# A perceiver layer on Trainium2: later tails' values half a section on, last output product half a step on, seven products of ones, root first

## The chip, the cores and the metric

The kernel runs on one core of a Trainium2 chip (trn2). All arithmetic is fp32. The metric is the device time in microseconds (us), median of three runs. Beside it there is one profiled execution, in which the hardware profiler records the instructions of each engine. The engines are TensorE (PE: matmuls, and PEld: its weight loads), VectorE (DVE), ScalarE (ACT), GpSimd (POOL) and SyncE (SP), which only issues DMAs here. ACT and POOL issue DMAs too, besides their own work.

## The reference

One layer in three stages, each on a layer norm of the running rows x (8 batches x 64 queries, 512 wide) and added to them:

```python
def stablemax(s):
    s = where(s >= 0, s + 1, 1 / (1 - s))
    return s / s.sum(-1)

# 1: cross attention, 16 heads of 32, context of 8 x 1601 rows of 512
n = layernorm(x)
q, k, v = n @ Wq.T + bq, ctx @ Wk.T + bk, ctx @ Wv.T + bv
x = x + (stablemax(q @ k.T / sqrt(32)) @ v) @ Wo.T + bo
# 2: causal self attention over 64 rows, 8 query heads of 64, one shared key and value
n = layernorm(x)
x = x + softmax(causal(n @ aWq @ (n @ aWk).T * 512**-0.5)) @ (n @ aWv) @ Wp + bp
# 3: experts, 512 -> 2048 -> 512
n = layernorm(x)
shared = mean over 2 of gelu(n @ sW1 + sb1) @ sW2 + sb2
gates = n @ rW + rb        # top 2 of 8, softmax over the two
x = x + shared + sum over the top 2 of w_e * (gelu(n @ W1[e] + b1[e]) @ W2[e] + b2[e])
```

## The kernel before

**Context.** The keys and values of the 8 x 1601 context rows are the larger part of the work. Each batch has three *sections* of 512 rows (24 in all, numbered 0 to 23), 64 further rows (its *tail*) and one last, *odd* row. A product of two 2x2 block matrices is made with seven block products instead of eight: `weight_parts` (L353, on DVE) makes the sums of weight blocks, `context_part` and `tail_parts` those of the context blocks (POOL), `multiply` (L370, its matmul is L376) issues one of the seven, and `products` (L382) returns the seven as *units*. A unit ends with a copy from PSUM on ACT (through a helper that keeps ACT's order, so the profile gives L87), a join on DVE (L405) or, for the fifth, an add on POOL (L448). The first section's keys are plain products (`first_keys`, L465).

**Tails.** They are taken for four batches at a time, because four tails of 64 rows fill a tile of 256. Half 0 (batches 0 to 3) is made at the start; half 1 after section 14, the last of batch 4. `load_tails` (L183) loads the context, `tail_parts` makes the block differences, `tail_products` (L536) returns the units: key units `ku`, value units `vu`, and the last value unit `last`, which also writes the values to a scratch in DRAM (`vt_d`, L559, on SP). `load_vt` (L568) reads a batch's values back when its scores begin. `odd_rows` (L501) and `odd_turn` (L522) make key and value of the odd rows; `odd_k` is filled by four ACT activations that add the key bias.

**The order of work.** `Plan` (L52) holds units, each with a planned length, and other steps, each with a planned time. The units run through: sections (loop at L1124), first expert, further expert blocks. Steps such as loading a section, scores and weighing of a tile of context are put in by their times. From this one program order, a scheduler orders each engine's instructions; PE, ACT, DVE, POOL and SP each run their own in order and wait for each other by semaphores.

**The chains.** When two batches are weighed, their 128 query rows form a *tile* (four in all). For each, `chain(tt)` (L728) lists the steps: `project` (output product of the cross attention, PSUM name ps_wo, L738, then the row statistics), `factors` (a root on ACT with `eps_t` as its bias, then a reciprocal), `apply` (normalise; loads of the attention weights awkv, awq and bias abp on SP), `turn`, `keys` (ps_akv, L775), `queries` (ps_aq, L788), `scores`, `exps`, `flip` (pt_s, L833), `values`, `output` (ps_ap), `factors`, `apply2`, `rows` and `gate`. The loop at L1226 gives each step its time: a gap of 5.0 us of plan times a step's width, and for the last tile 3.2 times at most 1.

**What stands beside the last chain.** While the last tile's chain runs, PE has the last products of the first expert (y, L1111) and then the hidden units of half-sized blocks (`SharedHalves`): seven products each for two quarters of an expert's hidden width (ps_hh, L376), with copies on ACT (L969), joins on DVE (L953) and GELU on ACT (L947). Below, the seven are counted from the first; the second and third need sums of weights that DVE makes (sw, L353). Then come their second products (ps_hr). The routed experts start with ps_h at L1640.

**The start.** DMAs of the first section (SP) and of the key weights wk (ACT's queue, five issues), then of wv and wq (ACT's queue); meanwhile PE makes products of ones (L246), whose result nobody reads.

Of the kernel before, what the change touches and what calls it, by code (L numbers as in the profile page):

```python
# [10 lines left out]
F32 = mybir.dt.float32  # L11
U32 = mybir.dt.uint32
I32 = mybir.dt.int32
AF = mybir.ActivationFunctionType
ALU = mybir.AluOpType
# [3 lines left out]
P = 128  # L19
B, SQ, E = 8, 64, 512  # L20
SKV = 1601
NT = B * SQ
NTT = NT // P
NC = E // P
H1, HD1 = 16, 32
NG = H1 // 4
# [12 lines left out]
NSEC = SKV // SEC  # L39
# [56 lines left out]
def perceiver_kernel(  # L96
# [7 lines left out]
    nc = tc.nc  # L104

    act = InOrder(tc, nc.scalar)

    def pool(name, bufs, **kw):
        return ctx.enter_context(tc.tile_pool(name=name, bufs=bufs, **kw))

    const = pool("const", 1)
# [20 lines left out]
    def at4(name):  # L132
        return atp.tile([P, 1024], F32, tag="at", name=name)
# [7 lines left out]
    def psa(name):  # L141
        return ps_a.tile([P, 512], F32, tag="a", name=name)
# [33 lines left out]
    def right_parts(x, n=SEC):  # L176
        return {"b11": x[:, 0:2, 0 : n // 2], "b12": x[:, 0:2, n // 2 : n],
                "b21": x[:, 2:4, 0 : n // 2], "b22": x[:, 2:4, n // 2 : n]}

    ROUND = TAIL - 1  # L180
    NQB = B // 2
# [26 lines left out]
    def bias_cols(src, n, name):  # L208
        t = const.tile([P, n], F32, name=name)
        nc.gpsimd.dma_start(out=t, in_=src)  # L210
        return t
# [6 lines left out]
    bk_t = bias_cols(bk, NC, "bk_t")  # L218
# [17 lines left out]
    make_identity(nc, ident)  # L236
    eps_t = const.tile([P, 1], F32, name="eps_t")
    nc.vector.memset(eps_t, EPS)
    one_t = const.tile([P, 1], F32, name="one_t")
    nc.vector.memset(one_t, 1.0)  # L240
    ones = const.tile([P, P], F32, name="ones")
    nc.vector.memset(ones, 1.0)

    ps = psa("ps_one")
    for _ in range(9):
        nc.tensor.matmul(ps[:, :P], ones, ones, start=True, stop=True)  # L246

    qT = big.tile([P, NG, NT], F32, name="qT")
# [81 lines left out]
    plan = Plan()  # L330
# [3 lines left out]
    PROD = FULL / 2  # L334
# [10 lines left out]
    def weight_parts(w, name):  # L345
        parts = {"a11": w[:, 0:2, 0:256], "a12": w[:, 2:4, 0:256],
                 "a21": w[:, 0:2, 256:512], "a22": w[:, 2:4, 256:512]}
        t = w8(name).rearrange("p k (c f) -> p k c f", c=2)
        for k in range(4):
            parts[f"s{k + 1}"] = t[:, k]  # L350
        for d, a, b, op in (("s1", "a21", "a22", ALU.add), ("s2", "s1", "a11", ALU.subtract),
                            ("s3", "a11", "a21", ALU.subtract), ("s4", "a12", "s2", ALU.subtract)):
            weight_parts.last = nc.vector.tensor_tensor(parts[d], parts[a], parts[b], op)  # L353
        return parts
# [135 lines left out]
    odd_k = const.tile([P, NG, B], F32, name="odd_k")  # L490
# [31 lines left out]
    def odd_turn():  # L522
        pt = psa("pt_odd")[:, : NG * B].rearrange("p (g b) -> p g b", g=NG)
        for g in range(NG):
            nc.tensor.transpose(
                pt[:, g, :], odd_rows.keys[0:B, g * P : (g + 1) * P], ident[0:B, 0:B]
            )
        for g in range(NG):
            act.activation(odd_k[:, g, :], pt[:, g, :], AF.Identity, bias=bk_t[:, g : g + 1])

    def tail_parts(h):
        p = tparts["t", h]
        for d, a, b in RIGHT:
            nc.gpsimd.tensor_tensor(p[d], p[a], p[b], ALU.subtract)

    def tail_products(h):  # L536
        def keys():
            kT = tlp.tile([P, NG, NQB, TAIL], F32, name="kTt", bufs=1)
            tails["odd", h] = kT[:, :, :, ROUND:TAIL].rearrange("p g b o -> p g (b o)")
            for k in range(NQB):  # L540
                tails[h * NQB + k, "k"] = kT[:, :, k, :]
            return kT

        def values():
            v = tails["v", h] = at4("vh").rearrange("p (k e) -> p k e", k=2)
            return v

        ku = products(
            ("t", h), True, dst=keys, hf=P,
            fit=lambda ps: ps.rearrange("p k (b s) -> p k b s", s=ROUND),  # L550
        )
        vu = products(("t", h), False, dst=values, hf=P)

        def last():
            vu[-1]()
            nc.gpsimd.tensor_copy(tails.pop(("odd", h)), odd_k[:, :, h * NQB : (h + 1) * NQB])
            v = tails.pop(("v", h))
            for k in range(NQB):
                nc.sync.dma_start(  # L559
                    out=vt_d[h * NQB + k, 0:ROUND, :],  # L560
                    in_=v[(k % 2) * ROUND : (k % 2 + 1) * ROUND, k // 2, :],
                )

        if h:
            return ku + vu[:-1] + [last]
        return ku[:2] + vu[:2] + ku[2:] + vu[2:-1] + [last]

    def load_vt(b):  # L568
# [32 lines left out]
    def weigh_bq():  # L601
        nc.vector.tensor_scalar_mul(bqs_t, bq_t, Q_SCALE)
# [521 lines left out]
    for i, (b, k) in enumerate(secs):  # L1124
        if i == 0:
            plan.add(4 * FULL, first_keys)
            there[i] = plan.now


            def early():  # L1130
                tail_parts(0)
                wkp.update(weight_parts(wk, "sk"))
                wvp.update(weight_parts(wv, "sv"))
                early.done = weight_parts.last
                weigh_bq()

            def sums_q():
                with tc.issue_after(Norm.last.ins):
                    wqp.update(weight_parts(wq, "sq"))

            plan.at(0.05, early)
            plan.add(2.0, odd_rows)
            for k, u in enumerate(tail_products(0)):
                if k == 2:
                    plan.add(0.3, odd_turn)
                plan.add(PROD / 2, u)
            for tt in range(NTT):
                plan.add(0.5, lambda tt=tt: first_rows(tt, early.done))
            plan.at(plan.now, sums_q)
            for n in range(4):  # L1150
                plan.at(plan.now + 0.01 * n, lambda n=n: context_part("q", n))
            tparts[0] = right_parts(cxs[0])
            values0 = products(0, False)
            for u in values0[:2]:
                plan.add(PROD, u)
            for u in products("q", True, wqp, qT, Q_SCALE, bqs_t):
                plan.add(PROD, u)
            asked = plan.now
            for n in range(4):
                plan.at(asked - 9.0 + 1.5 * n, lambda n=n: context_part(0, n))  # L1160
            for u in values0[2:]:
                plan.add(PROD, u)
            for tt in range(NTT):
                plan.at(plan.now + 4.0 * tt, lambda tt=tt: add_bo(tt))
            plan.add(0.0, act.bind)
        else:
            for u in products(i, True):
                plan.add(PROD, u)
            there[i] = plan.now
            for u in products(i, False):  # L1170
                plan.add(PROD, u)

        last = len(plan.units)
        if i + 1 < len(secs):
            start = plan.now - 14 * PROD
            if i == 0:
                plan.at(0.1, lambda: load_cx(1))
                for n in range(4):
                    plan.at(plan.now - 8.0 + 2.0 * n, lambda n=n: context_part(1, n))
            else:  # L1180
                plan.at(start + 0.1, lambda i=i: load_cx(i + 1))
                for n in range(4):
                    plan.at(plan.now - (6.5 - 1.5 * n) * PROD, lambda i=i, n=n: context_part(i + 1, n))
        if k == NSEC - 1:
            if b == NQB:
                plan.at(plan.now - 30.0, lambda: load_tails(1))
                plan.at(plan.now - 15.0, lambda: tail_parts(1))
                for u in tail_products(1):
                    plan.add(PROD / 2, u)
    end = plan.now  # L1190
    step = (end - 14.0) / len(tiles_in)
# [12 lines left out]
    wide = [len(UNITS[u]) for _, u in units]  # L1204
# [21 lines left out]
    for tt in range(NTT):  # L1226
        gap = 5.0 if tt < NTT - 1 else 3.2
        for bb in range(2):
            b = 2 * tt + bb
            last = (b + 1) * nu - 1  # L1230
            done = weighed[last]

            more = 2.0 if b < B - 1 else 0.0
            plan.at(min(when[last] + 2.4 * step, done) + more, lambda b=b: sums(b))
            plan.at(done + 1.0 + 1.5 * more, lambda b=b: finish(b))
        pre, steps = chain(tt)
        for fn in pre:
            plan.at(done - 10.0, fn)
        time = done + 1.0
        for fn, wide in steps:  # L1240

            time += gap * (wide if tt < NTT - 1 else min(wide, 1))
            if fn in asks and tt < NTT - 1:

                time = min(t for t in when if t >= time - 8.0) + 6.0
            plan.at(time, fn)
# [560 lines left out]
```

## Time and profile before

| | us |
|---|---|
| median of 3 runs (1356.39 to 1356.93) | 1356.39 |
| profiled execution | 1357.59 |
| its span, first to last instruction | 1355.9 |
| PE busy | 1340.1 |
| DVE / POOL / ACT busy | 971.0 / 764.3 / 674.6 |
| PE busy in 0 to 40 | 37.76 |
| PE busy in 500 to 560 (later tails) | 58.28 |
| PE busy in 860 to 960 (last tile's chain) | 97.44 |

The mean granted clock of PE is 0.998. Lines in the profile are those of this kernel. A row such as `PE L376 MATMUL ps_k<-cxt,wk 128*128 128x128 f32 x16` is a group of sixteen passes on PE at line 376, with output and inputs by the program's names; an fp32 matmul is recorded as two passes. In brackets stands the idle time of the engine just before, and what ended it.

### The profile page before, as it was taken

Reading aid. Unit: us, or ns where it says so; the run is one execution under the profiler, and the core shown is the slowest. Engines: PE = TensorE matmul, PEld = TensorE weight load, DVE = VectorE, ACT = ScalarE, POOL = GpSimd, SP = SyncE. Lnnn points to the kernel's source line nnn. Section 1 sums busy time; section 2 is a strip of 40 time slices with the busy share of each in tenths; the row PEclk is TensorE's granted clock in tenths of the full one; section 3 lists DMA queues with packets and bytes.
Section 4 is the critical chain, followed back from the end, with each engine's and each line's share of the span. In section 5 each row is a group of like instructions: output and inputs, shape, how many; then the busy total and the mean of one; then the engine's idle time right before and its main releaser. Section 6 shows DMA issues by size and latency. Waiting matters only on the chain.

```text
span 1355.9 us, 37790 instructions
## 1 busy us (share of the span) xinstructions
PE 1340.1 (99%) x16590; PEld 1121.9 (83%) x16590; DVE 971.0 (72%) x868; ACT 674.6 (50%) x1432; POOL 764.3 (56%) x686
## 2 busy tenths in 40 slices
PE   9999999999999999999999999999999999999997
PEld 6888888888788888878888877588898999977786
DVE  3499999998999997999998999887876200010314
ACT  4466666665666665766666667335222211122230
POOL 3789899888978986988889877600200000000020
PEclk9999999999999999999999999999999999999999
DMA  7211111122402122112113114436645936788721
GB/s 212 79 41 33 37 33 64 37 79 65 157 2 72 49 75 82 47 33 64 41 46 101 65 33 164 141 126 241 220 170 173 340 129 255 266 308 325 273 89 33
DMA packets 88280, 162.76 MB, mean 120 GB/s; under 512 B 13494, under 2 KB 15062, under 8 KB 88112
## 3 DMA queue, kind: packets, MB, share of 16 engines
q1 hardware_dynamic: 81232, 142.70, 31.1%
q0 software_dynamic: 4512, 13.92, 2.9%
q10 hardware_dynamic: 2368, 3.69, 0.9%
q8 instruction: 132, 2.16, 0.7%
q14 instruction: 36, 0.29, 0.1%
HBM read 148.50 MB, written 11.78 MB: 118 GB/s over the span
## 4 chain that ended last, share of the span: by engine, by line
PE 93%; DVE 3%; ACT 2%; POOL 1%; issue 1%; DVEq 0%; POOLq 0%; ACTq 0%
PE ps_k L376 22%; PE ps_v L376 21%; PE ps_h L1640 9%; PE ps_hh L376 7%; PE ps_hr L376 6%; PE ps_s L631 5%; PE y L1552 4%; PE y L1561 4%; PE ps_o L681 3%; PE ps_h L1099 2%; DVE neg L649 1%; PE y L1111 1%; PE ps_aq L788 1%; PE ps_k L465 1%; PE ps_wo L738 1%; PE ps_ap L860 1%
## 5 line engine op out<-in xcount | busy, mean ns | idle before, releaser
L649 DVE RECIPROCAL neg<-neg 128x512 f32<-128x512 f32 (+1 forms) x224 | 686.4, 3095 | 49.9 <-ACT neg L87 48.0
L650 POOL TENSOR_TENSOR at<-at,neg 128x512 f32<-128x512 f32 (+1 forms) x224 | 269.0, 1207 | 94.3 <-DVE neg L649 80.4
L662 POOL TENSOR_TENSOR tot<-tot,at 128x512 f32<-128x512 f32 (+1 forms) x176 | 224.9, 1278 | 13.1
L87 ACT ACTIVATE neg<-neg,one_t 128x512 f32<-128x512 f32 (+1 forms) x224 | 157.7, 704 | 0.0
L87 ACT ACTIVATE neg<-ps_s 128x512 f32<-128x512 f32 (+1 forms) x224 | 127.9, 571 | 56.9 <-PE ps_s L631 50.0
L1640 PEld LDWEIGHTS ps_h<-xgT,w1t 128*128 128x128 f32 x896 | 123.0, 191 | 27.8 <-issue 26.1
L87 ACT ACTIVATE at<-ps_s 128x512 f32<-128x512 f32 (+1 forms) x224 | 128.5, 573 | 23.5 <-PE ps_o L681 23.5
L1645 ACT ACTIVATE hT<-ps_h,b1e 128x128 f32<-128x128 f32 (+3 forms) x112 | 42.7, 381 | 194.8 <-PE ps_h L1640 194.8
L376 PE MATMUL ps_v<-sv,tx 128*128 128x256 f32 x576 | 132.5, 382 | 0.0
L1640 PE MATMUL ps_h<-xgT,w1t 128*128 128x128 f32 (+3 forms) x896 | 129.2, 287 | 0.0
L1543 POOL DMA_DIRECT2D ys_d<-yo x10 | 5.4, 544 | 219.6 <-DVE yo L1542 219.6
L376 PE MATMUL ps_k<-tx,sk 128*128 128x256 f32 x552 | 128.5, 384 | 0.6 <-DVE kT L405 0.6
L376 PEld LDWEIGHTS ps_v<-sv,tx 128*128 128x128 f32 x576 | 107.7, 190 | 17.6 <-issue 1.9
L376 PEld LDWEIGHTS ps_k<-tx,sk 128*128 128x128 f32 x552 | 102.7, 190 | 16.4 <-DVE kT L405 0.7
L87 ACT COPY v<-ps_v 128x512 f32<-128x512 f32 x96 | 56.6, 589 | 78.0 <-PE ps_v L376 77.9
L1534 DVE COPY xgT<-pt_x 128x512 f32<-128x512 f32 (+3 forms) x12 | 6.8, 593 | 119.4 <-PE pt_x L1533 119.4
L87 ACT ACTIVATE kT<-ps_k,bk_t 128x256 f32<-128x256 f32 (+1 forms) x142 | 60.9, 482 | 61.4 <-PE ps_k L376 54.9
L376 PE MATMUL ps_v<-wv,cx 128*128 128x256 f32 x384 | 89.4, 382 | 0.0
L376 PE MATMUL ps_k<-cx,wk 128*128 128x256 f32 x368 | 86.5, 383 | 0.0
L631 PEld LDWEIGHTS ps_s<-qT,kT 32*64 32x64 f32 x6144 | 70.4, 130 | 16.6 <-issue 14.4
L376 PEld LDWEIGHTS ps_v<-wv,cx 128*128 128x128 f32 x384 | 71.8, 190 | 10.8 <-issue 0.4
L631 PE MATMUL ps_s<-qT,kT 32*64 32x64 f32 x6144 | 77.4, 231 | 0.4 <-DVE v L405 0.4
(303 smaller groups left out, 2242.3 us busy)
## 6 DMA issues: line engine op xcount, KB each, us to landing
w1t<-in_W_dram SPq DMA_DIRECT2D x32, 1024.0 KB, 11.0
w2t<-in_W_dram SPq DMA_DIRECT2D x32, 1024.0 KB, 9.7
cx<-in_ctxT_dram SPq DMA_DIRECT2D x23, 1024.0 KB, 5.3
w1t<-in_sW_dram SPq DMA_DIRECT2D x14, 1024.0 KB, 6.3
w2t<-in_sW_dram SPq DMA_DIRECT2D x14, 1024.0 KB, 5.6
wo<-in_woT_dram SPq DMA_DIRECT2D x4, 1024.0 KB, 7.3
awq<-in_aWq_dram SPq DMA_DIRECT2D x4, 1024.0 KB, 7.2
awp<-in_aWp_dram SPq DMA_DIRECT2D x4, 1024.0 KB
```

The source lines that it names most:

```text
L87: ins = getattr(self.engine, name)(*args, **kw)
L376: nc.tensor.matmul(ps[:, k, :], l[:, c, k * P : (k + 1) * P], r[:, c, :], start=first and k == 0 and c == 0, stop=last and c == 1, skip_gr ...
L631: nc.tensor.matmul(ps[j][h, k, g, :], kT[rows, g, h], qT[rows, g, b * SQ : (b + 1) * SQ], start=True, stop=True, skip_group_check=True,)
L649: nc.vector.reciprocal(neg, neg)
L650: nc.gpsimd.tensor_add(pos, pos, neg)
L662: nc.gpsimd.tensor_add(tot, tot, at[:, :, i])
L681: nc.tensor.matmul(accs[b][32 * j : 32 * j + 32, g, :], v[:w, (4 * g + j) * 32 : (4 * g + j + 1) * 32], at[j // 2][:w, j % 2, k, g, :], st ...
L1099: nc.tensor.matmul(ps[:, :N0], w0[0, q][:, c, r * P : (r + 1) * P], shared_x["x"][:, c, :N0], start=c == 0, stop=c == NC - 1,)
L1552: nc.tensor.matmul(self.y[k], hT[:, s : s + w], w2t, start=first, stop=last)
L1561: nc.tensor.matmul(y[d // 2][:, d % 2, :], w2t[:, d * P : (d + 1) * P], hT[:, : self.n], start=first and d % 2 == 0, stop=last, skip_group ...
L1640: nc.tensor.matmul(ph[:, : blk.n], w1t[:, c, f : f + P], blk.x[:, c, :], start=c == 0, stop=c == NC - 1,)
L1645: nc.scalar.activation(hT[:, : blk.n], ph[:, : blk.n], AF.Gelu, bias=blk.bias(hc))
```

## The change

- `root_t`: a new one-element-per-partition tile, the root of `eps_t`, made on ACT directly after the setting of `eps_t`. Nobody reads it. On ACT it comes after the five issues of wk and before those of wv and wq.
- Seven products of ones instead of nine.
- `odd_turn`: one DVE addition with the key bias broadcast, in place of four ACT activations.
- `tail_products(1)` returns key units and value units apart. The key units stay after section 14; the value units, with the writes to `vt_d`, come between the keys and the values of section 15.
- In the loop of the last chain, the first step (`project`) comes after 1.5 gaps instead of 1, so it and every later step of that chain are 1.6 us of plan later.

```diff
+    root_t = const.tile([P, 1], F32, name="root_t")
+    nc.scalar.activation(root_t, eps_t, AF.Sqrt)
...
-    for _ in range(9):
+    for _ in range(7):
         nc.tensor.matmul(ps[:, :P], ones, ones, start=True, stop=True)
...
-        for g in range(NG):
-            act.activation(odd_k[:, g, :], pt[:, g, :], AF.Identity, bias=bk_t[:, g : g + 1])
+        nc.vector.tensor_tensor(
+            odd_k, pt, bk_t.rearrange("p (g o) -> p g o", o=1).to_broadcast([P, NG, B]), ALU.add
+        )
...
         if h:
-            return ku + vu[:-1] + [last]
+            return ku, vu[:-1] + [last]
...
             for u in products(i, True):
                 plan.add(PROD, u)
             there[i] = plan.now
+            if i == (NQB + 1) * NSEC:
+
+                for u in later_values:
+                    plan.add(PROD / 2, u)
             for u in products(i, False):
                 plan.add(PROD, u)
...
-                for u in tail_products(1):
+                later_keys, later_values = tail_products(1)
+                for u in later_keys:
                     plan.add(PROD / 2, u)
...
-            time += gap * (wide if tt < NTT - 1 else min(wide, 1))
+            time += gap * (wide if tt < NTT - 1 else 1.5 if fn is steps[0][0] else min(wide, 1))
```

## The prediction

> **What bounds the kernel now.** I read the page first: its rows of engines and the chain that ended last.
>
> ```profile
> PE 1340.1 (99%) x16590; PEld 1121.9 (83%) x16590; DVE 971.0 (72%) x868; ACT 674.6 (50%) x1432; POOL 764.3 (56%) x686
> PE 93%; DVE 3%; ACT 2%; POOL 1%; issue 1%; DVEq 0%; POOLq 0%; ACTq 0%
> ```
>
> TensorE (PE) is busy 1340.1 of 1355.9 us and carries 93% of the chain; the granted clock is 0.998. So an edit pays only by taking PE work away or by closing a gap between PE instructions. Next I read PE's waits, with their totals:
>
> ```profile
> PE ps_akv L775 <- DVE kTt L405: 1.7, 1, 1.7
> PE ps_wo L738 <- POOL ctT L717: 1.6, 1, 1.6
> PE ps_one L246 <- DVE ones L242: 1.3, 1, 1.3
> PE ps_k L376 <- ACT kTt L87: 0.9, 1, 0.9
> ```
>
> Columns: total, times, longest. The first is at 516 us, around the later tails; the second at 882, the last tile's output product; the fourth at 28 us, in the first tails. The rest are 0.6 or less. The change has parts at all three places, so I read the timeline of the first 40 us and of 868 to 905 us. Columns: start, length, engine, line, and in brackets the idle time before.
>
> ```profile
> 1.30 4.21 PE L246 MATMUL ps_one<-ones 128*128 128x128 f32 x18 [1.30 <-DVE ones L242]
> 5.31 14.75 PE L465 MATMUL ps_k<-cx,wk 128*128 128x256 f32 x40
> 21.91 2.02 PE L376 MATMUL ps_k<-cxt,wk 128*128 128x128 f32 x16
> 24.39 0.73 ACT L87 ACTIVATE odd_k<-pt_odd,bk_t 128x8 f32<-128x8 f32 x4
> 25.37 0.37 ACT L87 COPY vh<-ps_v 128x256 f32<-128x256 f32 x1 [0.25 <-PE ps_v L376]
> 25.76 1.28 ACT L87 ACT_TABLE_LOAD   x1
> 27.05 0.48 ACT L87 ACTIVATE ln_rs<-ln_mv,eps_t 128x1 f32<-128x1 f32 x2
> 28.69 0.61 ACT L87 ACTIVATE kTt<-ps_k,bk_t 128x128 f32<-128x128 f32 x2
> 29.35 2.12 PE L376 MATMUL ps_k<-cxt,sk 128*128 128x128 f32 x16 [0.93 <-ACT kTt L87]
> ```
>
> The load of the root's table, two roots and a normalisation stand between ACT and the kTt copies that free PE's bank.
>
> ```profile
> 882.05 1.75 DVE L353 TENSOR_TENSOR sw<-w1t 128x512 f32<-128x512 f32 x2
> 883.33 0.94 POOL L717 TENSOR_TENSOR ctT<-rec,bv_t 128x256 f32<-128x256 f32 x1
> 883.73 1.09 DVE L353 TENSOR_TENSOR sw<-sw,w1t 128x512 f32<-128x512 f32 x1
> 884.33 3.70 PE L738 MATMUL ps_wo<-wo,ctT 128*128 128x512 f32 x8 [1.64 <-POOL ctT L717]
> 888.67 1.28 DVE L353 TENSOR_TENSOR sw<-w1t 128x512 f32<-128x512 f32 x2
> 890.24 1.28 ACT L87 ACT_TABLE_LOAD   x1
> 892.19 1.28 ACT L947 ACT_TABLE_LOAD   x1
> ```
>
> PE's work before ps_wo ends at 882.5; ps_wo waits for POOL to end at 884.27.
>
> **Seven products of ones.** Two 128x128 products are four passes fewer, 0.213 us each in the trace (matmul starts in the row at 1.30), so L465 starts at 4.45 instead of 5.31; its first keys chunk landed at 4.14. That is 0.85 earlier. But PE's clock turns at 7.0 in the trace (L465's 256-column passes are 0.427 apart before, 0.216 after). In the Trainium skill, "TensorE: Matmul & The Clock Gate", Part 1, warming up is a matter of time, not of the number of products. By that rule two more real passes run cold (2 x 0.21 lost) and 0.43 is left; by the row's spacing alone it would be 0.85. I take the rule. Then the gain meets a DMA: the tails' cxt landed at 21.78 for the product that starts at 21.91, and PE would be there at 21.5. So nothing is left of it (bounds -0.4 and +0.2, if the clock turns later).
>
> **Root first, odd keys on DVE.** ACT's load (1.28) goes from 25.76 to the start, where ACT idled until 10.41. There it stands behind the five wk issues and ahead of the issues of wv and wq on ACT's queue, so wv is issued at about 6.0 instead of 4.54. wv landed at 18.14, behind wk's chunks, and DVE used it at 18.17; I take the delay as hidden by the queue behind wk, at up to +0.5 if it isn't. The four odd_k activations (0.73) become one DVE instruction of some 0.2 (an estimate: the 128x128 keys join of 256 columns takes 0.41), between two row statistics.
>
> Were ACT's 2.01 all the story, the wait at 28 (1.09 between the ends of matmuls) would go whole. It doesn't: in the changed program's instruction order the kTt copies stand behind two normalisations (xn), not one, and these hang on DVE: last statistics (res landed 25.36), odd_k, a kTt join, two reciprocals. I get ln_nb at 27.0, xn at 27.05 and 27.77 (spacing 0.72), kTt 28.5 to 29.1, PE at 29.15 instead of 29.35. One values product fills in ahead of the next keys product and gives about 0.2 more. Sum **-0.4** (bounds -1.1, the whole wait; +0.5, one more xn in front).
>
> **Later values apart.** The same seven products, half a section (seven planned products, 12 us) later. The PE order up to ps_akv is unchanged, so its 1.65 wait for DVE's kTt join stays. Afterwards section 15's keys come before the values. SP then issues the next cx load ahead of the four vt_d writes and the vt reads; those are wanted some 14 us later (near 570 in the trace), so this costs nothing, and up to 0.5 if vt comes late. What goes is DVE starving between 522 and 538 (idle 1.19, 0.73, 3.04, 3.57), but only 0.2 of that reached PE, plus small POOL and DVE waits between 552 and 663 that sum to 1.2. I take **-0.3** (bounds -1.4, all of these; +0.5).
>
> **The output product half a step on.** PE is at 882.52 and now goes on with hidden products of the shared expert (0.87 each, 3.73 for 16 passes). This closes the wait of 1.81 if these are ready. The first is. The second needs DVE's second weight sum, which ended at 884.82: PE stands 1.46. The next needs ACT's copy of the first: 0.63 more. So 2.09 of waits take the place of 1.81, and ps_wo starts at 888.2, 3.84 later. "SBUF — State Buffer", on who interferes, says that DVE's two-input SBUF operations and GpSimd lock each other out of a shared port. The row agrees: the pair of sums took 1.75 at 882.05, with POOL running, and 1.28 at 888.67. Its weight is against this edit: the sums are slow exactly while PE needs them. At 1.28 and 0.68 they would end at 884.0, with 0.8 less stall; ctT's POOL work is in the same place after the change, so I keep the slow ones.
>
> Everything behind ps_wo moves with it. On SP that is the attention weights (awkv, abp, awq, awp), issued at 867.8 to 876.3 in the trace and first used at 900.2: landing took 5.6 to 7.2 on the page, so they have over 15 us to spare, and the new order puts awq and awp first; nothing. The root's and the GELU's table loads (2 x 1.28) now come before ACT's copy of the fourth product, on which another hidden product waits: copy at 900.3, stall 1.53. The skill's "ScalarE: Activation LUTs", on what a table load costs, adds 1.38 of drain to each; at 25.76 the load starts right behind a copy and ln_rs right behind the load, 1.3 in all, so I take the row. By the page the stall would be 2.8 longer, 4.3. The copy xnT_a stands behind ten GELUs (0.32 each): stall 0.5 at the last ps_akv. Against these, two waits of before go: pt_s on DVE (0.62) and part of ps_hh on DVE (0.3); the one at pt (0.62) becomes 0.8 at a rows product. Together +0.28 +1.53 +0.5 -0.62 -0.3 +0.18 = 1.57. The 1.53 is the least certain term: at 890.24 the root's load ran while ACT waited for DVE's ln_mv, and where it does so again one of the two loads costs PE nothing. Between 0.25 and 1.53 I take the middle, 0.9, which makes the sum **+0.9** (bounds -1.8, only the fill works; +2.6, the stalls whole with DVE one sum later).
>
> **Sum.** 0 - 0.4 - 0.3 + 0.9 = +0.2. The profiled execution took 1357.59, 1.69 around its span of 1355.9; its span becomes 1356.1. The runs' median is 1356.39, 1.2 below that execution, so I add the difference to the median: **1356.6**.
>
> **Rivals.** (1) All three waits go: the DVE sums are in time once DVE's order changes, and ACT is free at 28. -1.1 -0.4 (ones) -1.0 -1.8 = -4.3, 1352.1. For it: PE is the bound, and each wait has one named releaser that the edits touch. Against: the instruction order puts another ACT or DVE result in front of PE at two places. (2) Slower: ACT's queue at 895 to 900 us. The last tile's ln_rs stands in front of the hidden copies; it waits for ln_mv, which came 3.8 after ps_wo's end in the trace (888.03 to 891.84) behind two weight sums. If it comes 1.9 later still, ACT holds the copy that long and the change costs over 2.7; with two more sums and a join (3 x 0.7) and xnT_a late in turn, +3.6, 1360.0. For it: ACT and DVE work in order, and DVE is full there. Against: PE has other products for some of the time. (3) The change doesn't do what it says: each wait is replaced by an equal one (cxt's DMA, DVE's sum, the unchanged ps_akv): 1356.4.
>
> **How the numbers follow.** 0.2%, 2.7 us, is about what a measurement of this kernel can tell from no change; all PE gaps of the span sum to only 11.7. My sum 0.47, rival 1 0.25, rival 2 0.18, rival 3 0.10. The likeliest's own range is 1354.0 to 1358.6 (about half of the summed bounds -4.7 and +3.8). The range for 8 in 10 reaches to the two outer cases, 1352.3 to 1360.0. Faster by over 0.2% (under 1353.7): most of rival 1, 0.22, and 0.02 of my sum: 0.24. Slower (over 1359.1): 0.16 of rival 2 and 0.03: 0.19. Within: 0.57.
>
> **What would show it.** Start: cxt's product still at 21.9; the kTt wait at 28 near 0.9, with one table load before 30. Later tails: ps_akv's wait of 1.7 unchanged; DVE's idle at 522 to 538 gone. Last tile: no wait of ps_wo on ctT, but about 1.5 of ps_hh on DVE sw and 1.5 on an ACT copy; the experts' first ps_h (L1640) at 953 to 954 instead of 952.64. I am wrong if the gaps at 882 to 901 sum to under 1.5 (rival 1) or over 5 (rival 2), or if a DMA (wv, vt) appears among PE's waits.

## The result and the profile after

The changed kernel took 1359.93 us (median of 11 runs, 1358.01 to 1363.72) against 1356.93 for the kernel before in the same runs: a ratio of 1.0025, 95% interval 1.0018 to 1.0033. It is slower by about 3.4 us. The forecast was 1356.6 and no measurable difference; the time lies at the slow end of the range for 8 in 10 (1352.3 to 1360.0), outside the likeliest sum's own (1354.0 to 1358.6). The profiled execution took 1361.72, with a span of 1360.1.

PE's rows of the page, and the first of PE's waits (total, times, longest):

```profile
PE 1340.7 (99%) x16586; PEld 1123.3 (83%) x16586; DVE 971.9 (71%) x869; ACT 673.1 (49%) x1428; POOL 764.2 (56%) x686
```

```profile
PE ps_hr L379 <- DVE res L1067: 2.0, 2, 1.5
PE ps_hh L379 <- ACT hq L973: 1.8, 2, 1.3
PE ps_s L635 <- issue: 1.7, 1, 1.7
PE ps_akv L779 <- DVE kTt L408: 1.7, 1, 1.7
PE ps_hh L379 <- DVE sw L356: 1.4, 1, 1.4
```

PE has as much work as before. The waits of before on ctT (1.6) and on ACT's kTt (0.9) are gone; the one at ps_akv stands as it was; five new ones of 0.5 to 1.5 belong to the last tile's chain, and one of 1.7 has no releaser at all ("issue"). Lining up the two profiles at the same piece of work gives where the time went (us from the span's start):

| piece of work | before | after | after minus before |
|---|---|---|---|
| scores with a short pause, PE | 145.04 | 143.31 | -1.73 |
| scores in front of the pause without releaser | 663.45 | 661.55 | -1.90 |
| gate of the third tile | 833.69 | 835.38 | +1.69 |
| last group of y ahead of ps_wo | 879.84 | 881.52 | +1.68 |
| first routed ps_h | 952.64 | 957.93 | +5.29 |
| last products | 1345.49 | 1349.25 | +3.76 |

So there are four terms: a gain of 1.9 by 661 us, nearly all of it at the start; a loss of 3.6 at 663 to 669; a loss of 3.6 between 880 and 958; and a gain of 1.5 behind 958. The last can't be put down to the change: that stretch took 391.3 us in the changed kernel, with the later values alone and with seven ones alone, and 391.9 to 397.6 in the other profiles, where waits of up to 3.0 near 975 or 990 us come and go with no one edit.

**The start.** The timeline of the changed kernel (start, length, engine, idle time in brackets):

```profile
4.34 1.28 ACT L241 ACT_TABLE_LOAD   x1 [4.34 <-DMA wk<-in_wkT_dram]
7.31 0.39 ACTq L156 DMA_DIRECT2D wv<-in_wvT_dram  x1
9.53 8.66 SPq L225 DMA_DIRECT2D res<-in_x_dram  x4
21.41 2.05 PE L379 MATMUL ps_k<-cxt,wk 128*128 128x128 f32 x16
22.05 1.32 DVE L305 BATCH_NORM_STATS2 ln_st<-res 128x6 f32<-128x512 f32 x2 [0.76 <-DMA res<-in_x_dram]
24.09 0.17 DVE L531 TENSOR_TENSOR odd_k<-pt_odd,bk_t 128x32 f32<-128x32 f32 x1
25.49 1.52 ACT L87 ACTIVATE xn<-res,ln_nb,ln_rs 128x512 f32<-128x512 f32 x2 [0.22 <-DVE ln_nb L314]
26.92 0.60 ACT L87 ACTIVATE kTt<-ps_k,bk_t 128x128 f32<-128x128 f32 x2
27.79 1.95 PE L379 MATMUL ps_k<-cxt,sk 128*128 128x128 f32 x16
```

The kTt copies do stand behind two normalisations, but these start at 25.49, not at 27.05: the rows of x (res) arrived earlier, with their first statistics at 22.05 instead of 23.38, and the roots no longer wait for a table load at 25.76. The issues on SP show where the rows got ahead:

```profile
13.73 5.55 SPq L225 DMA_DIRECT2D res<-in_x_dram  x4
```

That is the kernel before; after the change SP issues the first rows at 9.53. SP works in order, and most of what it waits for ahead of the rows is the landing of context loads (cx, cxt). wv, on ACT's queue, was issued at 7.31 instead of 4.54, so in between it took nothing from these loads; that this is why they landed earlier is argued from the order. wv was still used at 18.18, as before (18.17). Over all sixteen profiles the first statistics start at 22.43 to 23.38 in the eight kernels without the early root, and at 20.68 to 22.61 in the eight with it. No wait is left at 28.

**The last tile.** The timeline of the changed kernel:

```profile
884.21 1.05 PE L379 MATMUL ps_hh<-xnT,w1t 128*128 128x128 f32 x8
886.65 1.13 PE L379 MATMUL ps_hh<-xt,sw 128*128 128x128 f32 x8 [1.40 <-DVE sw L356]
888.25 1.16 PE L379 MATMUL ps_hh<-xt,sw 128*128 128x128 f32 x8 [0.46 <-ACT hq L973]
890.13 3.60 PE L742 MATMUL ps_wo<-wo,ctT 128*128 128x512 f32 x8
897.73 1.28 ACT L87 ACT_TABLE_LOAD   x1
899.34 1.28 ACT L951 ACT_TABLE_LOAD   x1
900.63 1.28 ACT L951 ACTIVATE hq<-hq,b_t 128x128 f32<-128x128 f32 x4
901.82 0.35 ACT L973 COPY hq<-ps_hh 128x256 f32<-128x256 f32 x1
902.22 1.16 PE L379 MATMUL ps_hh<-xnT,sw 128*128 128x128 f32 x8 [1.34 <-ACT hq L973]
907.97 0.70 PE L379 MATMUL ps_hr<-sw,ht 128*128 128x256 f32 x2 [1.53 <-DVE res L1067]
```

ACT's copy at 901.82 stands behind two table loads, a root and four GELUs, and PE waits for it. The rows product at 907.97 waits for DVE, whose sums of hidden values wait for the same late GELUs. Between the starts of matmuls, the stalls here are 1.56, 0.63, 1.51 and 1.69, and 0.68 at 945: 6.07, against 1.80, 0.62 and 0.62 (3.04) before. The other 0.6 of the 3.6 are pauses of up to 0.15 where long and short products alternate more often.

**The pause without a releaser.** The same kernel, around 663 us:

```profile
659.59 1.89 PE L379 MATMUL ps_k<-cx,wk 128*128 128x256 f32 x8
661.97 1.41 PE L635 MATMUL ps_s<-qT,kT 32*64 32x64 f32 x107 [0.20 <-DVE v L408]
665.07 0.35 PE L635 MATMUL ps_s<-qT,kT 32*64 32x64 f32 x9 [1.69 <-issue]
665.35 3.42 PE L379 MATMUL ps_k<-cx,wk 128*128 128x256 f32 x8
```

PE stops inside a run of scores, in which it waits for nobody. The next eight passes take 3.42 instead of 1.89: the granted clock is 0.50 for 3.41 us from 665.75. The DMA packets in the trace suggest what PE lacked. One of the two instruction queues moves 131 packets of 16 KB here, one per some 255 of PE's 33391 records, so I read each as a page of PE's instructions. The page due here was fetched at 662.73, 19.7 us after the last; in the profile of before at 657.31. Just ahead of it stands a load of context:

```profile
658.10 0.37 SPq L169 DMA_DIRECT2D cx<-in_ctxT_dram  x1
```

Its packets moved from 659.12 to 662.72; the page's came 0.01 later. In the profile of before the page came 3.7 ahead of the same load's first packet (661.02).

### The profile page after: what moved, and what is told of

It reads as the page before. It is cut to its first block, busy times and chain, and to the rows that moved or that the text cites. A ratio compares the mean times of both kernels' runs of the same rounds, so it can differ in the third digit from the quotient of the medians.

```text
span 1360.1 us, 37771 instructions
## 1 busy us (share of the span) xinstructions
PE 1340.7 (99%) x16586; PEld 1123.3 (83%) x16586; DVE 971.9 (71%) x869; ACT 673.1 (49%) x1428; POOL 764.2 (56%) x686
## 4 chain that ended last, share of the span: by engine, by line
PE 92%; DVE 3%; ACT 2%; POOL 1%; issue 1%; DVEq 0%; ACTq 0%; POOLq 0%
PE ps_k L379 21%; PE ps_v L379 21%; PE ps_h L1650 9%; PE ps_hr L379 7%; PE ps_hh L379 7%; PE ps_s L635 5%; PE y L1562 4%; PE y L1571 4%; PE ps_o L685 3%; DVE neg L653 2%; PE ps_h L1103 2%; PE y L1115 1%; PE ps_aq L792 1%; PE ps_k L468 1%; PE ps_ap L864 1%; PE ps_wo L742 1%
```

## Experiments

Each kernel was timed against the kernel before on the same chip. There were four such groups; in them the kernel before had medians of 1356.55 (first four rows), 1356.41 (next four), 1357.54 (next three) and 1358.82 (last three). So ratios can be compared across rows, and times only within a group. "Whole range" is from the lowest to the highest single time.

| kernel | ratio to before, 95% interval | whole range, us |
|---|---|---|
| the three edits of the start | 0.9997 (0.9989 to 1.0005) | 1355.10 to 1359.10 |
| later values apart | 0.9997 (0.9988 to 1.0005) | 1355.03 to 1357.98 |
| output product later | 1.0028 (1.0018 to 1.0038) | 1359.15 to 1361.47 |
| all but the output product | 1.0005 (0.9995 to 1.0014) | 1354.70 to 1361.22 |
| seven ones alone | 1.0004 (0.9995 to 1.0013) | 1354.22 to 1360.28 |
| root and odd keys | 0.9995 (0.9986 to 1.0003) | 1354.96 to 1356.94 |
| start, nine short ones | 0.9995 (0.9986 to 1.0004) | 1354.61 to 1356.71 |
| output product alone later | 1.0023 (1.0013 to 1.0032) | 1357.96 to 1363.11 |
| output product at 1.3 gaps | 1.0047 (1.0032 to 1.0063) | 1360.56 to 1367.42 |
| before, no root there | 1.0016 (1.0007 to 1.0025) | 1357.47 to 1362.65 |
| output product later, no root there | 1.0005 (0.9996 to 1.0014) | 1356.67 to 1359.76 |
| whole change, nine short ones | 1.0028 (1.0019 to 1.0038) | 1360.15 to 1363.68 |
| all but the output product, nine short ones | 0.9988 (0.9979 to 0.9997) | 1356.31 to 1357.93 |
| start with nine short ones, output product behind one hidden product | 1.0025 (1.0014 to 1.0036) | 1360.77 to 1363.80 |

### Which part costs

First the parts by themselves, each edit as in the diff of the change. The start:

> Only the three edits of the start (seven ones, root first, odd keys on DVE). Theory (the last tile's later output product costs, the start gains): about 1.8 us faster than before, 0.9986 to 0.9990 of it, because in the changed kernel the wait at 28 us was gone and the work at 143 us stood 1.73 earlier; the granted clock and the waits behind 143 us as before. Rival (the start's gain is an accident of one execution, or is given back where section loads now come earlier): within 0.5 us of before.

The later values:

> Only the later tails' values half a section on. Theory: within 0.5 us of before, with the wait of 1.7 at ps_akv unchanged. Rival (this edit shifts PE's instruction pages so that one is late, the 1.7 us stall without a releaser at 663 us of the changed kernel's profile): 2 to 4 us slower, with that stall near 665 us again.

The output product:

> Only the last tile's output product half a step later. Theory: about 3.6 us slower than before (1.0022 to 1.0032), with stalls near 1.5 on DVE's weight sum, 0.6 and 1.4 on ACT's copies and 1.6 on a rows product between 882 and 910 us, in place of the 1.8 on ctT. Rival (the loss lies in the late instruction page, not here): within 1.5 us of before.

And all but the output product:

> All of the change but the later output product. Theory: 1.5 to 2.3 us faster than before (0.9983 to 0.9989), the last tile's chain as before. Rival (late instruction page in this kernel as well): 1 to 3 us slower than before, with the page's stall in its profile.

The output product costs, alone and in full: 1.0028, with 76.40 us from the last group of y to the first routed ps_h, as in the changed kernel (76.41), against 72.80 before and 72.79 in the kernel with all but this edit. Its stalls are those of the changed kernel to 0.02, and its profile has no late page, so the loss is this edit's own. The later values cost nothing measurable; the wait of 1.7 is there. The start's gain is smaller in the runs than in one profile (0.9997 where 0.9986 to 0.9990 was expected; the rival, within 0.5 us, came true): two profiles with these edits (alone, and with the later values) still had 0.48 and 0.94 of stall at 28 us, with first statistics at 22.61 and 22.60 instead of 22.05. And all but the output product was not faster, a miss for both theories: its profiled execution was, at a span of 1353.7, but single times reached 1361.22. Still the parts sum to the whole within the noise: 0.05% and 0.28% slower, against 0.25% (0.18% to 0.33%).

### The start, edit by edit, and PE's pages

In the profile of the kernel with only the start's edits the pause without a releaser was there again (1.52, at 663.55), followed by the half clock again. These kernels have fewer products of ones, so every later PE instruction lies elsewhere in its page; they also do everything earlier. To tell the two apart, the count was to be put back and the time kept:

```diff
-    for _ in range(7):
-        nc.tensor.matmul(ps[:, :P], ones, ones, start=True, stop=True)
+    for _ in range(9):
+        nc.tensor.matmul(ps[:, :100], ones, ones[:, :100], start=True, stop=True)
```

The time was not kept. Nine products of 100 columns took 4.16 us, as nine whole ones did (4.21), where seven took 3.36, and the product behind them starts at 5.25 (5.31 before, 4.45 with seven). So these kernels put back the count and, with it, the 0.8 us. The ones alone:

> Only seven products of ones instead of nine. Theory (PE's instruction pages shift by the products left out, and the page that PE needs at 663 us then comes late in some executions): between 0.5 faster and 0.8 slower than before in the median, some single times 2 to 3.5 us above the kernel's lowest; where the profiled execution has it, a stall of 1.5 to 1.9 without a releaser near 663 to 665 us. Rival (the late page is chance, the same for every kernel): 0.4 us faster, no more spread than before.

Root and odd keys, with nine full ones:

> Root first and odd keys on DVE, with nine products of ones. Theory: 0.9 to 1.4 us faster than before, since the wait at 28 us shrinks by 0.6 to 1.1 and the tails start earlier; PE has no instruction less than before, so no stall near 663 us. Rival (the gain at the start is mostly the ones): within 0.5 us of before.

All three, with nine short ones:

> The three edits of the start, but with nine products of ones of 100 columns each (900 columns, as against 896 of seven whole ones): PE's time for them is that of seven, its number of instructions that of before. Theory of the pages: 1.3 to 1.9 us faster than before, and no stall near 663 us. Rival (the stall comes from the earlier times, not from the instruction count): as with seven, 0.4 to 0.9 us faster, with single times 2 to 3.5 us up.

The ones alone were no faster (1.0004), with single times up to 6.1 us above the lowest; their profile has no such stall. Root and odd keys gained 0.6 us and all three with nine short ones 0.8 (which differ only in columns that saved no time), less than their theories said, and both with an interval that reaches to no change; no single time of these two kernels stands more than 2.1 above the lowest, and no profile of them has the stall.

The time of the page separates the two counts without exception. Its fetch, counted from the start of the ps_k group in front of the pause (659.59 in the changed kernel):

| products of ones | profiles | page fetched, us from the ps_k group |
|---|---|---|
| nine, full or short | 12 | -4.22 to -3.98 |
| seven | 4 | -1.65, +0.66, +2.94, +3.13 |

Both fetches near +3 stalled PE; the two earlier ones didn't. The late page therefore comes with the shifted instructions, not with the earlier times: with the root first and nine products, full or short, the ps_k group starts at 659.39 to 660.12, as early as with seven (659.59 to 660.08; before 661.49), and the page still came 4.0 to 4.2 ahead of it.

What may have held it back can be read beside the load of context. With nine products the page moved 3.5 to 3.8 us ahead of the load's first packet in all twelve profiles. With seven it moved 1.2 ahead of the first packet, 1.1 behind it, and twice at the load's end (0.14 before and 0.01 after its last packet); these two stalled PE. This is no single case. Between 40 and 860 us of the sixteen profiles a page starts 0.12 times per us on average; within loads of 450 packets and more, up to 0.5 us before their last packet, 0.06 times; around that last packet (from 0.5 before to 0.3 behind) 0.39 times. This is what pages would do that fall due during a large load and are moved only at its end; how the DMA engines choose between the two is not shown. Why two products fewer move the page by 2.5 us or more is not shown. The ones alone had the wait that the prediction had named, for the tails' context:

```profile
20.73 1.47 PE L376 MATMUL ps_k<-cxt,wk 128*128 128x128 f32 x11 [0.53 <-DMA cxt<-in_ctxT_dram]
```

The clock of that execution was full from 4.27 on, so PE was there early. Over the sixteen profiles this product starts between 20.73 and 21.95, with no order among the kernels; how much the ones are worth is set there and by the clock.

### Why the later output product costs

Only the product later, the steps behind it at their old planned times:

```diff
-            plan.at(time, fn)
+            plan.at(time + (1.6 if tt == NTT - 1 and fn is steps[0][0] else 0.0), fn)
```

> Only the last tile's output product 1.6 us of plan later; the later steps of that chain keep their planned times. Theory (what costs is that the normalisation's table loads and the copies behind it come later whenever ps_wo does): 2 to 3.8 us slower than before, with the stalls on DVE's weight sum and on ACT's copy as with the whole step. Rival (what costs is the later place of the steps behind): within 0.8 us of before.

1.0023, with stalls of 1.57, 0.63 and 1.51 at the same places: as the theory said, it isn't the planned time of the later steps. Next, ACT's root was left out in the last tile's first normalisation (its factor is then 1/(variance + eps), so the output differs), in the kernel before and with the later output product:

```diff
...
-            act.activation(self.rs, self.mv[:, 1:2], AF.Sqrt, bias=eps_t)
+            act.activation(self.rs, self.mv[:, 1:2], AF.Identity if self.plain else AF.Sqrt, bias=eps_t)
...
+            st["norm"].plain = tt == NTT - 1
```

> The kernel before, in which the last tile's first normalisation leaves out the square root (its factor is 1/(variance + eps)), so that ACT loads no root table there. Both theories: within 0.7 us of before, as the loads at 890 and 892 us lie beside PE work.

> The same omission of the square root together with the later output product (1.5 gaps). Theory (the root's and GELU's table loads ahead of the copy of the fourth product make the stall of 1.5 at 901 us, and through the GELUs that of 1.7 at 906): the stall at 901 shrinks below 0.4, that at 906 by about 1.3, and the kernel is 0.5 to 1.8 us slower than before, from the weight sum and the first copy. Rival (ACT's queue itself is too long, whatever it loads): as with the root, 3.2 to 4 us slower.

PE's waits between 880 and 955 us with the later product and without the root:

```profile
PE ps_hh L376 <- DVE sw L353: 1.4, 1, 1.4
PE ps_hr L376 <- DVE res L1064: 0.5, 1, 0.5
PE ps_hh L376 <- ACT hq L970: 0.5, 1, 0.5
```

and its ACT, which goes from the normalisation's factor (ln_rs, here without the root) to GELUs to copy with no table load between:

```profile
896.71 0.30 ACT L87 ACTIVATE ln_rs<-ln_mv,eps_t 128x1 f32<-128x1 f32 x1
897.00 1.28 ACT L948 ACTIVATE hq<-hq,b_t 128x128 f32<-128x128 f32 x4
898.18 0.35 ACT L970 COPY hq<-ps_hh 128x256 f32<-128x256 f32 x1
```

Both late stalls (1.51 and 1.68) are gone, and the way from y to ps_h is 73.19 us instead of 76.40. Without the later product the same omission shortens it only from 72.80 to 72.44. So some 3 us hang on the two table loads ahead of ACT's copies and GELUs. Compared with the kernel before without the root (72.44), 0.75 is left for the weight sum, the first copy and small pauses. In the runs, too, nothing of the later product's cost is left without the root: 1.0005 with it, 1.0016 at its old place. The latter kernel was itself slower than before, a miss for both theories: its profile has a stall of 2.08 at 973 us, in which ACT's copy came at 975.05, right behind a packet of the other instruction queue (8 KB, at 974.53). That ACT lacked instructions there is argued from this order alone.

Then less of the shift: the product after 1.3 gaps,

```diff
-            time += gap * (wide if tt < NTT - 1 else min(wide, 1))
+            time += gap * (wide if tt < NTT - 1 else 1.3 if fn is steps[0][0] else min(wide, 1))
```

> The kernel before with the last tile's output product after 1.3 gaps instead of 1 (1.5 in the change), and the later steps of that chain with it: the first hidden product stands ahead of it on PE, the two that need DVE's sums and ACT's copy stand behind. Theory (the loss comes from products that are not ready and from table loads ahead of ACT's copies): the wait on ctT shrinks from 1.8 to 0.9 and no wait on a weight sum is left, while copies and GELUs still stand behind the loads; between 0.9 faster and 1.5 slower than before. Rival (any shift of the chain costs the 3.6): 2.5 to 4 us slower.

The wait on ctT halved to 0.8 as expected and no weight sum was waited for; still it was the slowest of all, some 6.4 us, outside both expectations:

```profile
PE ps_akv L775 <- ACT xnT_a L87: 2.6, 1, 2.6
```

Here twelve GELUs, with a wait of 1.15 for a join of DVE among them, stand between the second table load and the copy xnT_a. The stall of 2.77 was followed by 6.83 us of half clock, and the way from y to ps_h is 78.21. In each order run here in which the loads stand ahead of what PE needs next, PE waited 1.5 to 2.8 us for it.

### What is left, and a faster version

> The whole change, but nine products of ones of 100 columns in place of seven of 128: PE's instruction count is that of before. Theory (the later output product costs 3.6, the start gives about 1.3, and the late page adds to the changed kernel in some executions): 1.8 to 2.8 us slower than before, less than the changed kernel's 3.4, PE's page at 655 us asked for about 6.1 us ahead of the landmark as in the other kernels with nine products, no stall near 663 us. Rival (the page has no part in the median): 3.0 to 3.8 us slower.

> All of the change but the later output product, with nine products of ones of 100 columns. Theory: 0.7 to 1.7 us faster than before, where the same kernel with seven products was not faster; no stall near 663 us. Rival (the page has no part): as with seven, within 0.7 us of before.

With all but the output product, nine short ones give 0.9988 (0.9979 to 0.9997): faster than the kernel before by some 1.6 us, as its theory said; its highest single time is 1357.93, where the kernel before has a median of 1358.82 on that chip. With the whole change they gave 1.0028, no better than seven: the expectation of less loss failed, and the rival came true. Its profile has no late page, but its span is 1360.6: the way from y to ps_h is 77.96, 1.6 longer than with seven, since the stall of 1.69 was followed by the half clock there. The windows view of that profile around the place (length, then busy PE, PEld, DVE, ACT and POOL with their counts, then the granted clock, DMA's share and GB/s):

```profile
903.00:906.00 3.00, 1.73 (x20) 1.14 (x20) 1.22 (x4) 0.01 (x1) 0.00 (x0) 1.00 0.83 320
906.00:909.40 3.40, 3.40 (x23) 2.71 (x22) 0.00 (x0) 0.27 (x1) 0.00 (x0) 0.50 0.03 6
```

Last, the product held behind exactly one hidden product, with the later steps of the chain where they were:

```diff
...
+            if tt == NTT - 1 and fn is steps[0][0]:
+                held.append(fn)
+            else:
+                plan.at(time, fn)
...
         for k, u in enumerate(blk.units()):
+            if held and k == 1:
+                plan.add(0.0, held.pop())
```

> The three edits of the start with nine products of ones of 100 columns, and the last tile's output product directly behind the first hidden product on PE, with the later steps of its chain at their old times. Theory (one ready product fills half of the wait on ctT, and the table loads stay ahead of fewer copies): wait on ctT 0.9 instead of 1.8, stalls behind it under 1, together 1 to 2.3 us faster than before. Rival (any product ahead of ps_wo moves the loads in front of a copy that PE needs): 0.5 faster to 2.5 slower, with a wait of over 1 us on ACT between 895 and 906 us.

The rival came true in its mechanism: the wait on ctT fell to 0.92, a stall of 1.51 came on a copy behind the table loads, and the way from y to ps_h stayed at 72.95. Its size, 1.0025 or 3.4 us, was outside both expectations. In its profile the rest comes later, from a stall of 2.99 at 973 us on another ACT copy and the half clock behind it; whether that belongs to the edit is not shown, since stalls of up to 2.08 stand there in kernels without it.

## Why the prediction was wrong, point by point

**The output product.** This is the step that failed: +0.9 was taken, and it measured +3.6 in the profile and 1.0028 (3.8 us) in runs of its own. The mechanism was right at the first three stalls: 1.46, 0.63 and 1.53 were predicted, and 1.56, 0.63 and 1.51 came. Two terms were mis-sized. "Between 0.25 and 1.53 I take the middle" gave away 0.6 on the ground that the root's load could run during ACT's wait for DVE; it didn't, for ACT was not waiting: ln_mv was ready at 897.56, before the load that began at 897.73. And the "stall 0.5 at the last ps_akv" was 1.69, at a rows product: I followed the late GELUs to the copy of xnT_a behind them, and not to DVE's sums of their results; that is 1.2. The small pauses, 0.6, had no term, and the 0.3 taken off for ps_hh on DVE lies at 978 us, behind this stretch. Together these are the 2.7 that were missing. Rival 2 named the place, ACT's queue with the last tile's root ahead of the copies, but a wrong trigger: DVE's mean was not later but came 3.8 after ps_wo's end, as before, and it was the table loads that held the copy. That its 1360.0 is almost the measured time is luck. The gaps from 882 to 901 summed to 3.7, between the two bounds that were to show me wrong: these left out the stall at 906, and ps_h at 956.2 (957.93 less the 1.7 by which the chain began later), against 953 to 954, was the sign that failed. The loads took 1.28 each, with ln_rs right behind the first: the row, not the page's longer price, was the right one. The weight of the port rule stayed small: after the change the two sums took 1.75 again, and the stall on them is in the sum.

**The start.** -0.4 was taken, with nothing for the ones; the runs of the three edits gave 0.9997, some 0.4, and the profile -1.73. In the profile 0.5 of it stands at the tails' first product (21.41 instead of 21.91, where cxt was to hold PE) and 1.56 at the product behind kTt (27.79 instead of 29.35). What was wrong in the way is "last statistics (res landed 25.36)": in the changed kernel the last statistics start at 24.18 and the first xn at 25.49, not 27.05. I had counted the delayed wv issue as a risk only, and had no term for an earlier x. wv was in time, as assumed, and cxt was not waited for at 21.41. The rule on warming up can be seen at work: over the sixteen profiles the full clock begins between 4.27 and 7.19 us, and with it and with cxt the tails' first product moves by 1.2, more than the ones were to gain.

**The later values.** -0.3 was taken; 0.2 came by 661 us, below what the runs can tell; the unchanged ps_akv wait was right. The small waits at 534 and 607 went, and one of 0.63 on DVE came at 565.

**What I had no step for.** That removing two products (eight of PE's records, 33391 instead of 33399) moves all later instructions within their pages was no part of the working. In the profiled execution it cost about 3.6 (1.86 of stall, 1.7 by the half clock behind it). And I counted each stall once, where the clock can add to it. The half-clock stretches ahead of the last product last 3.41, one 6.83, and each follows a stall of 1.5 to 3.0. "TensorE: Matmul & The Clock Gate" in the Trainium skill, Part 1, has a free-running window of 3413 ns, and all these stretches begin on a grid of that length, counted from the first full clock of their profile. Up to 1340 us, PE was idle for 45% or more of the window ahead of each of the twelve falls. All four windows with over half idle were followed by one; of the 22 with 45% to 50%, eight were. Nor does the place of the stall decide: that at ps_akv lies whole in one window, 48.4% idle, in the profile of before (no fall) as in that of the later values (a fall). Such a stall can cost 1.7 more, and what decides it is open.

A small reading was wrong too: the gaps of PE sum not to 11.7 but to 9.0 ahead of the last product's end, with 6.8 us behind it.

The account of the one profiled pair: -1.9 by 661, +3.6 for the page with its half clock, +3.6 for the product, -1.5 behind 958, which gives the +3.8 at the last products. In the medians the output product's own 1.0028 is enough for the measured 1.0025, and the rest of the change, 1.0005, can't be told from nothing. What page and half clock add to the medians is not settled: without the output product, nine short ones instead of seven went with 0.9988 against 1.0005; with it, with 1.0028 against 1.0025; and nine also start PE's work 0.8 later.

## What to carry to other kernels

Before filling a wait on the bound engine with later work, list what that work itself waits for, and follow the moved step through the in-order queues of the helping engines: a table load that lay beside the bound engine's work can land in front of its next copy. Expect instruction pages to move when instructions ahead of a long program are left out, look for the wait that has no releaser, and read in the trace that a control changed only what it was meant to: the shorter products here kept the count but saved no time. Price a stall of 1.5 us or more on the matmul engine with the clock that it may lose afterwards.

## What the runs showed of the hardware that was not expected

- Sixteen profiles, two groups: PE's instruction page near 655 us is fetched 4.0 to 4.2 us ahead of the same group of ps_k with nine products of ones, and between 1.65 ahead and 3.13 behind it with seven. Twice the page came at the end of a 1 MB load of context and PE stopped, for 1.52 and 1.86 us; the profile calls it "issue". Around the last packet of such loads pages start three times as often as on average (0.39 against 0.12 per us), and within them half as often (0.06).
- After stalls of 1.5 to 3.0 us, shorter than one stretch of the clock, the granted clock fell to 0.50 for 3.41 us (near 518, 666, 888, 906 or 976 us), and once for 6.83 (at 904). The same 1.8 us stall at ps_akv had it in five of sixteen profiles.
- In the eight profiles in which one 1 MB load (wv) is issued on ACT's queue at 7.31 to 8.62 instead of 4.19 to 4.67, its first use was 0.3 us later on average (16.73 to 18.78, against 17.33 to 18.17), and the first use of x 0.8 us earlier.
